# Neighbour sums with features on partitions, scores from one product, R in two rows

## The chip, the cores and the metric

The kernel runs on one core of a Trainium2 chip. The metric is the device time of one execution in microseconds (us), as the median of several runs; profiles come from one further execution that is recorded by the hardware profiler.

## The reference, cut to what matters

A node table `x` (3327 rows of 512 features) goes through four graph layers, each of the form `x = x + layer(relu(layernorm(x)))`. Layers 0, 2 and 3 are graph attention with 8 heads of 64 features. Layer 1 is a GraphSAGE layer.

```python
# attention (layers 0, 2 and 3; layer 0 ends in a batch norm, the others in an ELU)
Wh = h @ W                                  # per head: n x 64
e = leaky_relu(s_i[:, None] + s_j[None, :], 0.2)   # per head, scores of Wh
e = where(adj > 0, e, -9e15)
out = softmax(e, axis=j) @ Wh
# SAGE (layer 1)
mask = adj > 0
agg = mask @ h / maximum(deg, 1)
out = relu(concat([h @ W_self + b_self, agg @ W_nb + b_nb]) @ W_comb + b_comb)
```

The adjacency is sparse and skewed: a few nodes have many neighbours, most have few.

## The kernel before, in words

Nodes are padded to 3328, in 26 blocks of 128 (P) and 52 groups of 64 (GB). The kernel first reads the adjacency and makes, for each group of 64 output nodes, a list of the nodes that are a neighbour of any of them. The lists are cut into chunks of 128 indices: 22 chunks for the first group, then 15, 13, 12, 11, 10 and so on down to 5 and once 4, 359 in all (`CAPS`). Each chunk has a 128 x 64 mask. All sums over neighbours are then products over gathered rows: GpSimd gathers the 128 rows of a chunk from a table in DRAM (`gather`, L1019), and TensorE adds them up in PSUM.

**Attention** (`attend`, three times). exp(leaky_relu(a + b)) is written as a product of a per-node factor and a maximum, so that a weight is max(R_i, r_j), masked. R belongs to the output node and r to the gathered node. For each group, SP fetches one row of R, 8 heads x 64 nodes, into one partition (`fetch`, L1043 and L1044), and `spread` (L1052) copies it to all 128 partitions as a product with a row of ones: 1 x 128 stationary, 1 x 512 moving, f32. A unit is up to three chunks of one group. For each unit VectorE takes the maximum (L1120, into PSUM) and multiplies by the mask (L1127), and TensorE makes 8 products per chunk (L1141), one per head: the weights, 128 x 64, are stationary, the gathered values, 128 x 65 (64 features and a one that sums the weights), are moving. Two heads go to the two halves of the output partitions. In `attend` the orders of TensorE, VectorE and ScalarE are those of the code (`manual_schedule`); GpSimd and SP are ordered by the framework, and outside `attend` all engines are. After each unit `later()` moves older groups on and calls `tick` once.

**The projection of the next layer** makes the table: per block of 128 nodes, the normed block is transposed (p_ps, L710, with four relu activations into hT, L713), two score products follow (p_sd: L717 has hT stationary and 8 columns of WA moving and puts nodes on partitions, L719 has WA stationary and hT moving and puts the 8 heads on partitions, as R needs them), then h @ W (p_wh, L731). The row of a node is 8 x 65 values and 8 factors r. R is clamped, passed through exp, and written to `r_dram`, heads x nodes. `Projection` does this at the start, beside the reading of the adjacency (L593, L595, L597, with the scores in one PSUM bank, `sd`). `Following` does it beside SAGE (for layer 2) and beside attention 2 (for layer 3): `norm` in three steps and `rest` in four, and each `tick` makes one step of the oldest block that is ready. Its PSUM tiles rotate through two banks beside SAGE and through one beside attention 2.

**SAGE**: for each chunk, one product (L1376) has the mask, 128 x 64, stationary and the gathered row, 128 x 512, moving; the two groups of a block fill the two halves of the output partitions, nodes x features. ScalarE casts the masks (L1357). `ending` then works in steps, one per tick: ScalarE scales by one over the degree (s_ag, L1315), TensorE transposes the block with four products (a_ps, L1319) and ScalarE copies it (aT, L1321); TensorE multiplies by the folded weights (n_ps, L1325); VectorE adds the node's own part (L1330), applies relu and adds x (L1331), SP writes the result, and the projection's `begin` takes the block.

The lines that a sentence can't say:

```python
        if self.ready and next(self.ready[0], None) is None:
            self.ready.pop(0)
...
                nc.tensor.matmul(acc[u * GB : (u + 1) * GB, :], m, z, start=f, stop=l)
...
                    nc.tensor.matmul(rb, ones[0:1, :], rrs.pop(g), start=True, stop=True)
```

Of the kernel before, what the change touches and what calls it, by code (L numbers as in the profile page):

```python
# [23 lines left out]
F32 = mybir.dt.float32  # L24
BF16 = mybir.dt.bfloat16
I32 = mybir.dt.int32
I8 = mybir.dt.int8
U8 = mybir.dt.uint8
U16 = mybir.dt.uint16
AF = mybir.ActivationFunctionType  # L30
ALU = mybir.AluOpType
# [5 lines left out]
P = 128  # L37
H = 8
F = 64
D = H * F  # L40
KC = D // P
# [7 lines left out]
GB = 64  # L49
# [10 lines left out]
SMALL = 53.0  # L60
# [510 lines left out]
class Projection:  # L571
# [15 lines left out]
    def block(self, c):  # L587
# [4 lines left out]
        for kc in range(KC):  # L592
            nc.tensor.matmul(sd[:, :H], hT[:, kc, :], WA[wl][:, kc, H:], start=(kc == 0), stop=(kc == KC - 1))  # L593
        for kc in range(KC):
            nc.tensor.matmul(sd[:H, P : 2 * P], WA[wl][:, kc, :H], hT[:, kc, :], start=(kc == 0), stop=(kc == KC - 1))  # L595
        for kc in range(KC):
            nc.tensor.matmul(wh, hT[:, kc, :], self.Wt[:, kc, :], start=(kc == 0), stop=(kc == KC - 1))  # L597
        row = pp.tile([P, ROW], F32, name="v_row", tag="v_row", bufs=3)
        V = row[:, : H * (F + 1)].rearrange("p (h f) -> p h f", f=F + 1)
        nc.scalar.activation(V[:, :, F : F + 1], sd[:, :H].rearrange("p (h o) -> p h o", o=1), AF.Exp)  # L600
        nc.scalar.activation(row[:, H * (F + 1) :], sd[:, :H], AF.Exp, scale=-0.8, bias=self.cs["down"])

        rr = pp.tile([H, P], F32, name="r_row", tag="r_row", bufs=2)
        nc.vector.tensor_scalar(rr, sd[:H, P : 2 * P], -SMALL, SMALL, ALU.max, ALU.min)
        nc.scalar.activation(rr, rr, AF.Exp, scale=0.8, bias=self.cs["down"][:H])
        n = P // GB
        nc.sync.dma_start(
            self.r_dram[c * n : (c + 1) * n, :, :].rearrange("g h i -> h g i"), rr.rearrange("h (g i) -> h g i", i=GB)
        )
# [42 lines left out]


class Following:

# [14 lines left out]
    def tick(self):  # L670
        if self.ready and next(self.ready[0], None) is None:
            self.ready.pop(0)
        for g in list(self.early):
            hx = next(g)
            if hx is not None:
                self.early.remove(g)
                self.ready.append(self.rest(*hx))
# [28 lines left out]
    def rest(self, c, hx):  # L706
# [9 lines left out]
        for kc in range(KC):  # L716
            nc.tensor.matmul(sd[:, :H], hT[:, kc, :], WA[wl][:, kc, H:], start=(kc == 0), stop=(kc == KC - 1))  # L717
        for kc in range(KC):
            nc.tensor.matmul(sd[:H, P : 2 * P], WA[wl][:, kc, :H], hT[:, kc, :], start=(kc == 0), stop=(kc == KC - 1))  # L719
        row = pp.tile([P, ROW], F32, name="v_row", tag="v_row", bufs=2)  # L720
        V = row[:, : H * (F + 1)].rearrange("p (h f) -> p h f", f=F + 1)
        nc.scalar.activation(V[:, :, F : F + 1], sd[:, :H].rearrange("p (h o) -> p h o", o=1), AF.Exp)
        nc.scalar.activation(row[:, H * (F + 1) :], sd[:, :H], AF.Exp, scale=-0.8, bias=self.cs["down"])
        rr = pp.tile([H, P], F32, name="r_row", tag="r_row", bufs=2)
        nc.scalar.copy(rr, sd[:H, P : 2 * P])  # L725
        yield True

        nc.vector.tensor_scalar(rr, rr, -SMALL, SMALL, ALU.max, ALU.min)  # L728
        wh = self.psum.tile([P, D], F32, name="p_wh", tag="p_ps", bufs=self.pb)
        for kc in range(KC):  # L730
            nc.tensor.matmul(wh, hT[:, kc, :], self.Wt[:, kc, :], start=(kc == 0), stop=(kc == KC - 1))  # L731
        yield True
        nc.scalar.activation(rr, rr, AF.Exp, scale=0.8, bias=self.cs["down"][:H])
        n = P // GB
        nc.sync.dma_start(
            self.r_dram[c * n : (c + 1) * n, :, :].rearrange("g h i -> h g i"), rr.rearrange("h (g i) -> h g i", i=GB)
        )
        for h in range(H):
            nc.scalar.mul(V[:, h, 0:F], wh[:, h * F : (h + 1) * F], V[:, h, F : F + 1])  # L739
        nc.sync.dma_start(self.table[c * P : (c + 1) * P, :ROW], row.bitcast(I32))  # L740
        yield None

# [248 lines left out]
def sparse(ctx: ExitStack, tc: tile.TileContext, t: dict, out: bass.AP, WA, ls, cs, idx, rdeg, first):  # L991
# [32 lines left out]
    def attend(layer, table, r_dram, finish, tick=lambda: None, home=None):  # L1024
# [11 lines left out]
        with tc.tile_pool(name=f"fatt{layer}", bufs=2) as ap, tc.tile_pool(  # L1036
# [4 lines left out]
            def fetch(g):  # L1041
                if g < ls.G:
                    rr = ap.tile([1, H * GB], F32, name="r_one", tag="r_one", bufs=3)  # L1043
                    nc.sync.dma_start(rr, r_dram[g : g + 1, :, :].rearrange("g h i -> g (h i)"))  # L1044
                    rrs[g] = rr

            def spread(g):


                if g < ls.G:  # L1050
                    rb = aps.tile([P, H * GB], F32, name="r_bc", tag="r_bc", bufs=2)
                    nc.tensor.matmul(rb, ones[0:1, :], rrs.pop(g), start=True, stop=True)  # L1052
                    rbs[g] = rb.rearrange("p (h i) -> p h i", i=GB)
# [99 lines left out]
    def following(lx, layer, wl, W, pb=1):  # L1153

        table = dram.tile([NP, ROW], I32, name=f"table{layer}")
        r_dram = dram.tile([ls.G, H, GB], F32, name=f"r_dram{layer}")
        pp = lx.enter_context(tc.tile_pool(name=f"fproj{layer}", bufs=1))
        pps = lx.enter_context(tc.tile_pool(name=f"fproj_ps{layer}", bufs=1, space=PSUM))
        return Following(tc, cs, N, wl, W, WA, table, r_dram, pp, pps, pb)
# [24 lines left out]
    with ExitStack() as mx:  # L1184
# [128 lines left out]
        def ending(b, acc):  # L1313
            ag = gp.tile([P, D], F32, name="s_ag", tag="s_ag")
            nc.scalar.mul(ag, acc, rdeg[:, b : b + 1])  # L1315
            yield
            tp = gps.tile([P, KC, P], F32, name="a_ps", tag="a_ps")
            for kc in range(KC):
                nc.tensor.transpose(tp[:, kc, :], ag[:, kc * P : (kc + 1) * P], cs["ident"])  # L1319
            aT = gp.tile([P, KC, P], F32, name="aT", tag="aT")  # L1320
            nc.scalar.copy(aT, tp)  # L1321
            yield
# [6 lines left out]
            o = gp.tile([P, D], F32, name="s_o", tag="s_o", bufs=3)  # L1329
            nc.vector.tensor_tensor(o, ps, y[:, b, :], ALU.add)  # L1330
            nc.vector.scalar_tensor_tensor(o, o, 0.0, xr, ALU.max, ALU.add)  # L1331
# [16 lines left out]
        def load(i):  # L1348
# [3 lines left out]
            for u, kn in enumerate(parts[i][1]):  # L1352
                if kn is not None:
# [4 lines left out]
                    for k in range(n):  # L1358
                        gather(zt[:, k, :], h_dram, k0 + k)
                        zs.append((k, u, k0 + k, mf[:, k, :], zt[:, k, :]))  # L1360
            zs.sort(key=lambda x: x[:2])
# [3 lines left out]
        for i, (b, _, begins, stops) in enumerate(parts):  # L1365
            load(i + SAHEAD)
            if begins:
                acc = gps.tile([P, D], F32, name="sage_acc", tag="sage_acc")
            at = -1
            for r, u, k, m, z in loaded.pop(i):  # L1370
                if r != at:
                    at = r
                    tick()
                g = b * PG + u
                f, l = k == ls.first[g], k == ls.first[g] + CAPS[g] - 1
                nc.tensor.matmul(acc[u * GB : (u + 1) * GB, :], m, z, start=f, stop=l)  # L1376
            if stops:
# [14 lines left out]
def gnn_stack(tc: tile.TileContext, t: dict, out: bass.AP):  # L1392
    with ExitStack() as ctx:
# [8 lines left out]
        table = ldram.tile([NP, ROW + NP // WB // 2], I32, name="table0")  # L1402
        r_dram = ldram.tile([ls.G, H, GB], F32, name="r_dram0")
        idx = kp.tile([P, ls.n], I32, name="idx")
# [73 lines left out]
```

## Time and profile before

| what | value |
|---|---|
| median of 3 runs | 2994.06 us (2988.13 to 3010.09) |
| the profiled execution | 3035.44 us, its span 3033.2 us |
| busy over the span: PE, VectorE, ScalarE, GpSimd | 77%, 59%, 35%, 45% |
| mean granted clock of TensorE | 0.788 of full |
| gathers for attention, L1019 | 1077, 952 ns each, 1025.4 us |
| gathers for SAGE, L1019 | 359, 950 ns each, 341.2 us |
| maximum and mask, L1120 and L1127 | 405 each, 639.5 and 638.3 us |
| h @ W beside other work, p_wh L731 | 416 records, 215.3 us |
| n_ps L1325 | 208 records, 106.7 us |
| scores, p_sd L717 and L719 | 416 records each, 72.5 and 75.9 us |
| transposes p_ps L710 and a_ps L1319 | 208 and 104 records, 326 and 337 ns each |

In the profile's rows an engine is PE (TensorE's products), PEld (its weight loads), DVE (VectorE), ACT (ScalarE), POOL (GpSimd) or SP (which only issues transfers). A row of a group says: line, engine, operation, output <- inputs, for a product the shapes "stationary rows * stationary columns, moving rows x moving columns", the count, then busy time, mean ns of one, and the idle time of the engine just before, with what ended it. Ends of products are modelled by the profiler, and products overlap, so the busy time of a group is shorter than count x mean. A row of the waits says: engine, line, what it waited for, us in total, times, longest. A row of the timeline begins with start and length in us and ends with the idle time before, where there was one.

### The profile page before, as it was taken

Reading aid. Unit: us, or ns where it says so; the run is one execution under the profiler, and the core shown is the slowest. Engines: PE = TensorE matmul, PEld = TensorE weight load, DVE = VectorE, ACT = ScalarE, POOL = GpSimd, SP = SyncE. Lnnn points to the kernel's source line nnn. Section 1 sums busy time; section 2 is a strip of 40 time slices with the busy share of each in tenths; the row PEclk is TensorE's granted clock in tenths of the full one; section 3 lists DMA queues with packets and bytes.
Section 4 is the critical chain, followed back from the end, with each engine's and each line's share of the span. In section 5 each row is a group of like instructions: output and inputs, shape, how many; then the busy total and the mean of one; then the engine's idle time right before and its main releaser. Section 6 shows DMA issues by size and latency. Waiting matters only on the chain.

```text
span 3033.2 us, 55483 instructions
## 1 busy us (share of the span) xinstructions
PE 2335.1 (77%) x22046; PEld 1441.9 (48%) x22046; DVE 1797.3 (59%) x2124; ACT 1051.0 (35%) x3857; POOL 1376.2 (45%) x1464
## 2 busy tenths in 40 slices
PE   4767577878787786888988677888889757777775
PEld 2434244555554332333333355555665445656554
DVE  7657577778876910011111277777766367887886
ACT  1223112233334322344444313445666601223333
POOL 1000255556551046666554255555544056565553
PEclk9778788877778898799999767777777766676766
DMA  7563377776662746666655366666655166666664
GB/s 279 186 258 125 133 217 226 235 222 207 201 191 78 248 140 198 195 202 221 202 182 180 114 169 183 186 181 188 185 173 171 56 184 186 188 195 194 200 197 130
DMA packets 186637, 561.52 MB, mean 185 GB/s; under 512 B 35385, under 2 KB 40321, under 8 KB 183044
## 3 DMA queue, kind: packets, MB, share of 16 engines
q0 software_dynamic: 114880, 404.47, 45.4%
q1 hardware_dynamic: 68470, 148.32, 13.8%
q10 hardware_dynamic: 3022, 5.11, 0.5%
q8 instruction: 177, 2.90, 0.4%
q14 instruction: 88, 0.72, 0.1%
HBM read 498.42 MB, written 59.36 MB: 184 GB/s over the span
## 4 chain that ended last, share of the span: by engine, by line
PE 63%; issue 14%; ACT 5%; DVE 2%; another core or an unknown queue 2%; DMA 1%; POOL 1%; SPq 0%; DVEq 0%; ACTq 0%; POOLq 0%
PE facc L1141 29%; PE p_wh L731 7%; PE r_bc L1052 6%; PE sage_acc L1376 5%; PE n_ps L1325 3%; PE p_sd L719 2%; PE p_sd L717 2%; PE s_ps L1300 2%; PE fwx_ps L1218 1%; PE bmean_ps L1228 1%; PE p_ps L710 1%; ACT v_row L739 1%; POOL rows L1019 1%; PE a_ps L1319 1%
## 5 line engine op out<-in xcount | busy, mean ns | idle before, releaser
L1019 POOL DMA_INDIRECT rows<-table,idx x1077 | 1025.4, 952 | 1231.6 <-PE facc L1141 362.4
L1141 PE MATMUL facc<-rows,wgt 128*64 128x65 f32 x17232 | 953.3, 270 | 380.9 <-issue 342.1
L1141 PEld LDWEIGHTS facc<-rows,wgt 128*64 128x64 f32 x17232 | 826.1, 178 | 669.3 <-issue 556.4
L1127 DVE TENSOR_TENSOR wgt<-mx,mask 128x1536 f32<-128x1536 f32 (+1 forms) x405 | 638.3, 1576 | 174.4 <-PE facc L1141 82.4
L1120 DVE TENSOR_TENSOR mx<-r_bc,rows 128x1536 f32<-128x1536 f32 (+1 forms) x405 | 639.5, 1579 | 163.9 <-PE facc L1141 75.9
L1019 POOL DMA_INDIRECT z_rows<-h_dram,idx x359 | 341.2, 950 | 392.0 <-ACT hT L1297 139.2
L1079 ACT ACTIVATE fhp<-sums,rd 64x64 f32<-64x64 f32 x832 | 219.7, 334 | 146.9 <-DVE rd L1073 85.2
L1052 PE MATMUL r_bc<-r_one,fones 1*128 1x512 f32 x312 | 220.9, 793 | 15.8 <-DMA r_one<-r_dram 9.3
L731 PE MATMUL p_wh<-fWt,hT 128*128 128x512 f32 x416 | 215.3, 664 | 1.8 <-ACT r_row L725 1.8
L1376 PE MATMUL sage_acc<-z_rows,z_mask 128*64 128x512 f32 x718 | 208.4, 635 | 10.6 <-issue 6.2
L1069 ACT COPY sums<-facc 128x260 f32<-128x260 f32 x156 | 57.5, 368 | 405.8 <-PE facc L1141 344.9
L728 DVE TENSOR_SCALAR r_row<-r_row 8x128 f32<-8x128 f32 x52 | 11.8, 228 | 301.7 <-ACT r_row L725 183.7
L1112 ACT ACTIVATE mask<-on 128x192 uint8<-128x192 uint16 (+1 forms) x135 | 46.5, 344 | 394.9 <-DVE on L1106 202.6
L1330 DVE TENSOR_TENSOR s_o<-n_ps,bn_y 128x512 f32<-128x512 f32 x26 | 17.9, 687 | 209.9 <-PE n_ps L1325 185.4
L731 PEld LDWEIGHTS p_wh<-fWt,hT 128*128 128x128 f32 x416 | 85.3, 216 | 107.4 <-issue 101.6
L597 PE MATMUL wh_ps<-fWt,hT 128*128 128x512 f32 x208 | 124.7, 731 | 2.5 <-DVE v_row L610 2.5
L739 ACT ACTIVATE v_row<-p_wh,v_row 128x64 f32<-128x64 f32 x416 | 89.8, 322 | 80.4 <-PE p_wh L731 70.3
L1325 PE MATMUL n_ps<-fWx,aT 128*128 128x512 f32 x208 | 106.7, 651 | 5.1 <-ACT aT L1321 3.4
L1079 ACT ACTIVATE bn_y<-sums,rd 64x64 f32<-64x64 f32 x416 | 109.5, 333 | 2.4 <-DVE rd L1073 0.5
L1376 PEld LDWEIGHTS sage_acc<-z_rows,z_mask 128*64 128x64 f32 x718 | 51.0, 140 | 116.6 <-issue 103.0
L1300 PE MATMUL s_ps<-fWx,hT 128*128 128x512 f32 x208 | 95.8, 615 | 9.2 <-ACT hT L1297 9.2
L713 ACT ACTIVATE hT<-p_ps 128x128 f32<-128x128 f32 x208 | 54.6, 277 | 123.2 <-PE facc L1141 82.8
(191 smaller groups left out, 2153.8 us busy)
## 6 DMA issues: line engine op xcount, KB each, us to landing
adj_i<-in_adj SPq DMA_DIRECT2D x26, 1664.0 KB
table<-v_row SPq DMA_DIRECT2D x78, 264.0 KB
rows<-table,idx POOLq DMA_INDIRECT x1077
fin_x<-fx SPq DMA_DIRECT2D x52, 256.0 KB
ln_x<-in_x SPq DMA_DIRECT2D x26, 256.0 KB
bn_x<-in_x SPq DMA_DIRECT2D x13, 512.0 KB
fx<-bn_x SPq DMA_DIRECT2D x13, 512.0 KB
fsage_x<-fx SPq DMA_DIRECT2D x26, 256.0 KB
```

Of the source, the lines that this page charges most:

```text
L597: nc.tensor.matmul(wh, hT[:, kc, :], self.Wt[:, kc, :], start=(kc == 0), stop=(kc == KC - 1))
L731: nc.tensor.matmul(wh, hT[:, kc, :], self.Wt[:, kc, :], start=(kc == 0), stop=(kc == KC - 1))
L739: nc.scalar.mul(V[:, h, 0:F], wh[:, h * F : (h + 1) * F], V[:, h, F : F + 1])
L1019: nc.gpsimd.indirect_dma_start(out=dst, out_offset=None, in_=src[:, :], in_offset=bass.IndirectOffsetOnAxis(ap=idx[:, k : k + 1], axis=0))
L1052: nc.tensor.matmul(rb, ones[0:1, :], rrs.pop(g), start=True, stop=True)
L1079: nc.scalar.mul(hp[o0 : o0 + GB, h * F : (h + 1) * F], sm[mine, q, 0:F], rd[mine, q, :])
L1120: nc.vector.tensor_tensor(mx[:, :n], rbs[g].unsqueeze(1).to_broadcast(full), gt[:, :n, H * (F + 1) : ROW].unsqueeze(3).to_broadcast(full), ...
L1127: nc.vector.tensor_tensor(wt[:, :n], mx[:, :n], mk.unsqueeze(2).to_broadcast(full), ALU.mult)
L1141: nc.tensor.matmul(accs[g][v * GB : (v + 1) * GB, q * (F + 1) : (q + 1) * (F + 1)], wt[:, k, h, :], gt[:, k, h * (F + 1) : (h + 1) * (F + 1)],
L1300: nc.tensor.matmul(ps, hT[:, kc, :], Wx[:, 0, kc, :], start=(kc == 0), stop=(kc == KC - 1))
L1325: nc.tensor.matmul(ps, aT[:, kc, :], Wx[:, 1, kc, :], start=(kc == 0), stop=(kc == KC - 1))
L1376: nc.tensor.matmul(acc[u * GB : (u + 1) * GB, :], m, z, start=f, stop=l)
```

## The change

1. **SAGE's sums.** The gathered row is now stationary, four times 128 x 128, and the mask moving, 128 x 64; the sum comes out with features on partitions and nodes along the free dimension. The transposes of `ending` and the scaling in ScalarE are gone; the sum is copied from PSUM and used as it is. One over the degree is applied behind the product with the weights, where nodes are on partitions again, in the VectorE step that adds the node's own part.
2. **Scores.** One product with all 16 columns of WA gives both scores with nodes on partitions. R is clamped and passed through exp there, and split into two parts (`halves`): the value in TensorE's reduced f32 form, and what remains of it. A product with the identity transposes both, 128 x 16 to 16 x 128, and they are written to `r_dram`, which has two rows for each group now.
3. **R's spread.** `fetch` brings two rows to two partitions, and `spread` adds them up as it copies them, 2 x 128 ones by 2 x 512, both read as the reduced f32 form (`float32r`).
4. **Steps.** `rest` has six steps in place of four. A tick makes up to two steps when two blocks are ready, and begins the next block when one ends.

```diff
@@ Projection.block
-            nc.tensor.matmul(sd[:, :H], hT[:, kc, :], WA[wl][:, kc, H:], start=(kc == 0), stop=(kc == KC - 1))
-        for kc in range(KC):
-            nc.tensor.matmul(sd[:H, P : 2 * P], WA[wl][:, kc, :H], hT[:, kc, :], start=(kc == 0), stop=(kc == KC - 1))
+            nc.tensor.matmul(sd[:, : 2 * H], hT[:, kc, :], WA[wl][:, kc, :], start=(kc == 0), stop=(kc == KC - 1))
...
+        sf = pp.tile([P, H], F32, name="s_col", tag="s_col", bufs=2)
+        nc.vector.tensor_scalar(sf, sd[:, :H], -SMALL, SMALL, ALU.max, ALU.min)
+        rs = halves(nc, pp, self.cs, sf)
+        nc.tensor.transpose(sd[: 2 * H, P : 2 * P], rs(), self.cs["ident"])
+        rr = pp.tile([2 * H, P], F32, name="r_row", tag="r_row", bufs=2)
+        nc.scalar.copy(rr, sd[: 2 * H, P : 2 * P])
...
+def halves(nc, pool, cs, sf):
+    rf = pool.tile([P, H], F32, name="r_full", tag="r_full", bufs=2)
+    rs = pool.tile([P, 2, H], F32, name="r_half", tag="r_half", bufs=2)
+    nc.scalar.activation(rf, sf, AF.Exp, scale=0.8, bias=cs["down"])
+    nc.scalar.copy(rs.bitcast(F32R)[:, 0, :], rf)
+
+    def other():
+        nc.vector.tensor_tensor(rs.bitcast(F32R)[:, 1, :], rf, rs[:, 0, :], ALU.subtract)
+        return rs.rearrange("p t h -> p (t h)")
+
+    return other
...
@@ Following.tick
-        if self.ready and next(self.ready[0], None) is None:
-            self.ready.pop(0)
+        for _ in range(min(2, len(self.ready))):
+            while self.ready and next(self.ready[0]) is None:
+                self.ready.pop(0)
@@ Following.rest
...
+        rs = halves(nc, pp, self.cs, sf)
         for h in range(H):
             nc.scalar.mul(V[:, h, 0:F], wh[:, h * F : (h + 1) * F], V[:, h, F : F + 1])
         nc.sync.dma_start(self.table[c * P : (c + 1) * P, :ROW], row.bitcast(I32))
+        yield True
+        tr = self.psum.tile([2 * H, P], F32, name="p_tr", tag="p_ps", bufs=self.pb)
+        nc.tensor.transpose(tr, rs(), self.cs["ident"])
+        yield True
+        rr = pp.tile([2 * H, P], F32, name="r_row", tag="r_row", bufs=2)
+        nc.scalar.copy(rr, tr)
...
@@ attend
-                    rr = ap.tile([1, H * GB], F32, name="r_one", tag="r_one", bufs=3)
-                    nc.sync.dma_start(rr, r_dram[g : g + 1, :, :].rearrange("g h i -> g (h i)"))
+                    rr = ap.tile([2, H * GB], F32, name="r_two", tag="r_two", bufs=3)
+                    nc.sync.dma_start(rr, r_dram[g, :, :, :].rearrange("t h i -> t (h i)"))
...
-                    nc.tensor.matmul(rb, ones[0:1, :], rrs.pop(g), start=True, stop=True)
+                    nc.tensor.matmul(rb, ones[0:2, :].bitcast(F32R), rrs.pop(g).bitcast(F32R), start=True, stop=True)
@@ SAGE, ending
-            ag = gp.tile([P, D], F32, name="s_ag", tag="s_ag")
-            nc.scalar.mul(ag, acc, rdeg[:, b : b + 1])
-            yield
-            tp = gps.tile([P, KC, P], F32, name="a_ps", tag="a_ps")
-            for kc in range(KC):
-                nc.tensor.transpose(tp[:, kc, :], ag[:, kc * P : (kc + 1) * P], cs["ident"])
             aT = gp.tile([P, KC, P], F32, name="aT", tag="aT")
-            nc.scalar.copy(aT, tp)
+            nc.scalar.copy(aT, acc)
...
-            nc.vector.tensor_tensor(o, ps, y[:, b, :], ALU.add)
+            nc.vector.scalar_tensor_tensor(o, ps, rdeg[:, b : b + 1], y[:, b, :], ALU.mult, ALU.add)
@@ SAGE, sums
-                nc.tensor.matmul(acc[u * GB : (u + 1) * GB, :], m, z, start=f, stop=l)
+                for kc in range(KC):
+                    nc.tensor.matmul(
+                        acc[:, kc, u * GB : (u + 1) * GB],
+                        z[:, kc * P : (kc + 1) * P],
+                        m,
+                        start=begins,
+                        stop=(stops and kc == KC - 1 and (r, u) == last),
+                    )
+                    begins = False
```

## The prediction

> **What bounds the kernel now.** I read the page first: how full each engine is, then the chain of work that ended last, then the groups the change touches.
>
> ```profile
> span 3033.2 us, 55483 instructions
> ...
> PE facc L1141 29%; PE p_wh L731 7%; PE r_bc L1052 6%; PE sage_acc L1376 5%; PE n_ps L1325 3%; PE p_sd L719 2%; PE p_sd L717 2%; PE s_ps L1300 2%; PE fwx_ps L1218 1%; PE bmean_ps L1228 1%; PE p_ps L710 1%; ACT v_row L739 1%; POOL rows L1019 1%; PE a_ps L1319 1%
> ...
> L1141 PE MATMUL facc<-rows,wgt 128*64 128x65 f32 x17232 | 953.3, 270 | 380.9 <-issue 342.1
> ...
> L1052 PE MATMUL r_bc<-r_one,fones 1*128 1x512 f32 x312 | 220.9, 793 | 15.8 <-DMA r_one<-r_dram 9.3
> ...
> L1376 PE MATMUL sage_acc<-z_rows,z_mask 128*64 128x512 f32 x718 | 208.4, 635 | 10.6 <-issue 6.2
> ```
>
> TensorE (PE) rows head the chain, among them every product the change rewrites. An f32 product shows as two records: 156 R rows give x312. Then busy time by stage (first projection; attention 0; norm and own product; SAGE; attention 2; attention 3):
>
> ```profile
> 0.00:354.00 354.00, 236.08 (x1504) 140.89 (x1504) 235.99 (x448) 79.84 (x352) 9.57 (x28) 0.84 0.51 188
> 354.00:951.00 597.00, 456.61 (x5980) 305.86 (x5980) 457.12 (x463) 178.34 (x621) 340.01 (x359) 0.77 0.69 212
> 951.00:1123.00 172.00, 139.23 (x378) 63.05 (x378) 103.55 (x202) 55.43 (x97) 20.80 (x22) 0.91 0.48 162
> 1123.00:1713.00 590.00, 495.24 (x1749) 207.32 (x1749) 57.78 (x159) 239.77 (x991) 320.36 (x337) 0.90 0.60 186
> 1713.00:2426.00 713.00, 574.78 (x6589) 393.88 (x6587) 480.79 (x480) 336.39 (x1278) 343.08 (x359) 0.76 0.57 167
> 2426.00:3033.00 607.00, 433.18 (x5848) 330.86 (x5848) 462.13 (x374) 161.27 (x520) 342.32 (x359) 0.67 0.64 184
> ```
>
> After the two times come PE, weight load, VectorE, ScalarE and GpSimd busy, PE's clock, DMA share, GB/s. SAGE is PE's stage (495 of 590). Attention has no full engine, so I read PE's own waits there, in attention 3 (the line's gaps end by "issue", nothing visible):
>
> ```profile
> PE facc L1141 <- issue: 135.4, 267, 2.6
> PE facc L1141 <- DVE wgt L1127: 7.6, 2, 6.6
> ```
>
> PE hardly waits for VectorE; its 433 busy and 135 of gaps make up the stage. Last, PE's order in one late SAGE block:
>
> ```profile
> 1577.60 0.60 PE L710 MATMUL p_ps<-fident,ln_h 128*128 128x128 f32 x4
> 1578.13 1.08 PE L1376 MATMUL sage_acc<-z_rows,z_mask 128*64 128x512 f32 x4
> 1579.14 3.70 PE L1325 MATMUL n_ps<-fWx,aT 128*128 128x512 f32 x8
> 1582.67 0.95 PE L717 MATMUL p_sd<-WA,hT 128*128 128x8 f32 x8
> 1583.56 1.04 PE L719 MATMUL p_sd<-hT,WA 128*8 128x128 f32 x8
> 1584.53 1.08 PE L1376 MATMUL sage_acc<-z_rows,z_mask 128*64 128x512 f32 x4
> 1585.54 3.70 PE L731 MATMUL p_wh<-fWt,hT 128*128 128x512 f32 x8
> 1589.17 2.79 PE L1376 MATMUL sage_acc<-z_rows,z_mask 128*64 128x512 f32 x12
> 1597.09 1.11 PE L1319 MATMUL a_ps<-fident,s_ag 128*128 128x128 f32 x4 [5.12 <-ACT s_ag L1315]
> ```
>
> Rates follow: sage_acc (2.79 - 1.08) / 8 = 0.214 us a record; n_ps starts 3.53 before the next product, 0.44 a record. The same 512 columns cost sage_acc half, because two groups of 64 columns run side by side. p_sd L717 takes 0.89 / 8 = 0.11.
>
> **What the Trainium skill says.** "TensorE: Matmul & The Clock Gate", section "LDWEIGHTS (loading the stationary operand)": the load costs about columns / 1.2 ns, so 107 ns for 128; L717, with only 8 columns moving, shows 0.11. The same page, "Step-by-step: what each phase is for": weight loads are pulled ahead of running matmuls; the trace agrees for 512 moving columns (0.44 is all moving time), none shows it for a 128-column load under 64. "FP8 and Floating Point Precision", "TensorE Precision Notes": true FP32 takes four passes, a reduced form reads FP32 as FP22. No row here shows that form.
>
> **The change, part by part.** All sums are against the profiled 3035.44 us (span 3033.2); the median of the runs is 41 lower, and I carry the difference over.
>
> 1. R spread (L1052), 52 per attention. Now 220.9 / 156 = 1.42 us each. One pass of four is an estimate of 0.36, with 0.1 for a fixed part, assumed, 0.45: saved 0.97 x 156 = 151 us of PE. Ends: 0 (it runs as now) and 1.15 each, 180. How much reaches the stage? Attention 2 does 115 + 86 + 19 = 220 us of projection products more than attention 3 and is 106 longer: 0.48. Attention 0 has 96 us of L1209, L1218 and L1228 more and is 10 shorter: 0. PE's waits say nearly 1. I take 0.65, -98; ends 0 and -180. VectorE's idle 140, 232 and 145 us leave room.
>
> 2. Scores in one product. L719 goes: 416 records, 75.9 us, split like the p_sd busy of the stages (59 and 86): 30 in SAGE, 45 in attention 2. L717 keeps its price, since loading sets it. One transpose a block comes back, at L710's 0.33 about 9 us a stage. Attention 2: (45 - 9) x 0.65 = -23.
>
> 3. The longer projection, six steps for four, two a tick when two blocks stand ready. In attention 2 PE's order is fixed by hand; in the changed order 17 blocks have the transposes directly before the scores, which then wait for four hT activations, 1.15 us in the trace, some 1.5 with latency (3.5 if ScalarE is inside the 2.14 us of L1079). Behind stand an R row and 24 facc products, which VectorE waits for. 17 x 1.5 x 0.65 = +17; ends 0 and +60. One block more is left for the tail, with one PSUM bank: 0.66 + 1.15 + 0.95 + 0.7 + 3.7 + 1.75 + 0.6, about +10. ScalarE, VectorE and SP gain small steps per block (0.2 to 0.3 each); ScalarE is at 240 of 590 and 336 of 713, so nothing; uncovered they are 1 us x 52.
>
> 4. SAGE's sums. Now 718 records side by side; then 359 x 4 x 2 = 2872 with 128-column loads: at 0.11 each 316 against 208, +108. Gone: 104 transposes, 22, and L719's 30; back: 9. Net +65. Two covers: the first two blocks hold 62 gathers, 62 x (0.95 + 0.30) = 78 us of GpSimd, more than their new PE work (62 x 8 x 0.11, and 8.4 of n_ps, p_wh, p_sd and p_ps a block, 71), so what they add (55, less 35 side-by-side pairs of 0.86) vanishes there, 24; and the transposes' waits for s_ag (41.7 us over 11, one shown above) go, since in the new order two chunks stand between the copy and n_ps. I count half, 21. Net +20; ends -30 and, if loads don't hide, +155. The fused VectorE step keeps 0.69.
>
> 5. First projection. PE loses 36 us (L595), but the stage waits on adjacency loads and VectorE's 3.6 us masks; the new chain clamp, exp, copy, subtract, transpose holds the sd bank longer. +5; ends -15 and +30. R's DMAs grow to 8 KB a block and 4 KB a fetch, under transfers of 264 KB: nothing; uncovered, a fetch a group late by some 0.1, 16 us.
>
> Sum: -98 - 23 + 17 + 10 + 20 + 5 = -69.
>
> **The rivals.** (A) Slower: weight loads don't hide under 64 columns, so a record costs 0.107 + 0.053 = 0.16: 2872 x 0.053 = 152, of which some 135 shows; 3060. For: no such pair in the trace. Against: facc, with 64-column loads, at times runs 96 records in 2.95 us, 0.031 each, which leaves no room for load and pass in turn. It decides from 0.135 a record on. (B) The gaps swallow it: facc's "issue" gaps come back as the R row shrinks, or the reduced product isn't shorter (the change then doesn't do what it says). The 187 us of parts 1 and 2 count 0.15 instead of 0.65, +93: 3018. For: attention 0 against 3. Against: the chain. (C) PE's saving counts in full and SAGE loses its waits: -187 + 26 + 10 - 15 = -166, 2828.
>
> **How the numbers follow.** Forecast 0.46, A 0.15, B 0.19, C 0.20. The likeliest is 2994 - 69 = 2925, its own range 2885 to 2970. The 8-in-10 range, 2838 to 3035, leaves out most of A and half of C. About 1% (30 us) is what a measurement of this kernel can tell from no change: faster 0.38 of the forecast and all of C, 0.58; same 0.08 and half of B, 0.17; slower A and half of B, 0.25.
>
> **What would show it.** R rows at x156 near 0.45 us, with the attention stages 20 to 45 shorter each; sage_acc at x2872 with busy near 316 and SAGE near 610; no wait for s_ag; in attention 2 some 1.5 us of PE idle before p_sd. A sage_acc pitch above 0.135, or facc gaps well over 342, would make the forecast wrong.

## The result, and the profile after

The changed kernel takes 3083.62 us, the kernel before 3000.98 beside it: ratio 1.028, 95% interval 1.023 to 1.033. It is 83 us slower where 69 us faster was forecast. First the page of the changed kernel: the span, TensorE's rows at the head of the chain of waits, and two groups.

```profile
span 3080.5 us, 58331 instructions
...
PE facc L1168 28%; PE sage_acc L1398 12%; PE p_wh L751 8%; PE n_ps L1346 4%; PE r_bc L1079 3%; PE p_sd L738 2%; PE s_ps L1327 2%; PE bmean_ps L1255 1%; PE fwx_ps L1245 1%; ACT fhp L1106 1%; ACT v_row L755 1%; PE p_ps L731 1%; ACT hT L734 1%; DMA fWc<-in_L_gnn_W_comb 1%
...
L1168 PE MATMUL facc<-rows,wgt 128*64 128x65 f32 x17232 | 982.3, 269 | 405.7 <-issue 378.8
...
L1398 PE MATMUL sage_acc<-z_mask,z_rows 128*128 128x64 f32 x2872 | 386.7, 296 | 12.2 <-issue 11.3
```

On the chain sage_acc went from 5% to 12% and R's spread from 6% to 3%. The 2872 records of sage_acc take 386.7 us, 71 more than forecast, and the gaps of facc grew from 342.1 to 378.8. The stages of the same execution follow (columns as in the prediction: length; busy PE, weight load, VectorE, ScalarE, GpSimd; clock, DMA share, GB/s), and then SAGE's row of the kernel before, cut at the same events:

```profile
0.00:302.80 302.80, 187.51 (x1298) 114.11 (x1298) 225.16 (x458) 87.92 (x403) 9.58 (x28) 0.84 0.58 216
302.80:912.50 609.70, 432.09 (x5953) 299.20 (x5953) 469.59 (x480) 180.10 (x623) 340.41 (x359) 0.79 0.69 211
912.50:1074.40 161.90, 130.86 (x365) 61.60 (x365) 100.62 (x199) 53.19 (x93) 15.14 (x16) 0.90 0.47 158
1074.40:1780.10 705.70, 651.86 (x3627) 513.82 (x3626) 63.55 (x186) 239.02 (x1021) 326.51 (x343) 0.84 0.53 158
1780.10:2477.30 697.20, 511.39 (x6351) 369.31 (x6352) 483.14 (x506) 340.71 (x1328) 342.36 (x359) 0.77 0.60 171
2477.30:3080.50 603.20, 415.48 (x5804) 337.35 (x5804) 462.03 (x374) 161.94 (x521) 343.97 (x359) 0.64 0.66 186
```

```profile
1116.20:1711.40 595.20, 500.44 (x1762) 209.93 (x1760) 58.47 (x160) 238.64 (x984) 322.26 (x339) 0.91 0.60 185
```

Cut at these events (first mean_ps of each layer, first var_ps, start of the last stretch of s_ps), the profile of before has 334.0, 619.2, 163.0, 595.2, 710.4 and 611.4 us. So SAGE lost 110, the first projection won 31, and the three attentions 31 together. The execution profiled before is 41 us slower than its median, and the fourth set of runs below gives the attentions only 13. SAGE's row holds the surprise: PE 151 us busier, and its clock 0.84 where it was 0.91.

The runs below were made in five sets, in which the kernel before took 2998, 2998, 2577, 3033 and 2577 us, and these levels do not follow the chip, since the chip of the first set and that of the fifth have the same number on record. Every ratio is to the kernel before in the same set. Stages are compared within a set, or between the two sets of 2998 where the text says so. The changed kernel itself was run with the result (3001 for the kernel before) and in the fourth set.

### The profile page after: what moved, and what is told of

Read it like the earlier page. It is cut to its first block, busy times and chain, and to the rows that moved or that the text cites. A ratio compares the mean times of both kernels' runs of the same rounds, so it can differ in the third digit from the quotient of the medians.

```text
span 3080.5 us, 58331 instructions
## 1 busy us (share of the span) xinstructions
PE 2329.2 (76%) x23394; PEld 1695.4 (55%) x23394; DVE 1804.1 (59%) x2202; ACT 1062.9 (35%) x3987; POOL 1378.0 (45%) x1464
## 4 chain that ended last, share of the span: by engine, by line
PE 64%; issue 14%; ACT 6%; DVE 2%; another core or an unknown queue 1%; DMA 1%; POOL 0%; SPq 0%; DVEq 0%; ACTq 0%
PE facc L1168 28%; PE sage_acc L1398 12%; PE p_wh L751 8%; PE n_ps L1346 4%; PE r_bc L1079 3%; PE p_sd L738 2%; PE s_ps L1327 2%; PE bmean_ps L1255 1%; PE fwx_ps L1245 1%; ACT fhp L1106 1%; ACT v_row L755 1%; PE p_ps L731 1%; ACT hT L734 1%; DMA fWc<-in_L_gnn_W_comb 1%
## 5 line engine op out<-in xcount | busy, mean ns | idle before, releaser
L1168 PE MATMUL facc<-rows,wgt 128*64 128x65 f32 x17232 | 982.3, 269 | 405.7 <-issue 378.8
L1398 PEld LDWEIGHTS sage_acc<-z_mask,z_rows 128*128 128x128 f32 x2872 | 380.8, 213 | 28.7 <-issue 28.2
L1398 PE MATMUL sage_acc<-z_mask,z_rows 128*128 128x64 f32 x2872 | 386.7, 296 | 12.2 <-issue 11.3
L751 PE MATMUL p_wh<-fWt,hT 128*128 128x512 f32 x416 | 241.1, 732 | 3.1 <-ACT s_col L745 1.4
L1351 DVE SCALAR_TENSOR_TENSOR s_o<-n_ps,rdeg,bn_y 128x512 f32<-128x512 f32 x26 | 19.5, 750 | 242.3 <-PE n_ps L1346 190.7
L751 PEld LDWEIGHTS p_wh<-fWt,hT 128*128 128x128 f32 x416 | 96.5, 243 | 115.9 <-issue 110.8
L738 PE MATMUL p_sd<-WA,hT 128*128 128x16 f32 x416 | 85.4, 322 | 58.5 <-ACT hT L734 45.7
L1378 ACT CAST z_mask<-mask 128x128 f32<-128x128 uint8 (+1 forms) x196 | 53.8, 295 | 206.8 <-PE sage_acc L1398 180.9
L738 PEld LDWEIGHTS p_sd<-WA,hT 128*128 128x128 f32 x416 | 82.0, 271 | 78.1 <-ACT hT L734 53.8
L1346 PE MATMUL n_ps<-fWx,aT 128*128 128x512 f32 x208 | 118.1, 710 | 6.4 <-issue 6.1
```

The costliest lines, as they stand in the source:

```text
L738: nc.tensor.matmul(sd[:, : 2 * H], hT[:, kc, :], WA[wl][:, kc, :], start=(kc == 0), stop=(kc == KC - 1))
L1168: nc.tensor.matmul(accs[g][v * GB : (v + 1) * GB, q * (F + 1) : (q + 1) * (F + 1)], wt[:, k, h, :], gt[:, k, h * (F + 1) : (h + 1) * (F + 1)],
L1346: nc.tensor.matmul(ps, aT[:, kc, :], Wx[:, 1, kc, :], start=(kc == 0), stop=(kc == KC - 1))
L1398: nc.tensor.matmul(acc[:, kc, u * GB : (u + 1) * GB], z[:, kc * P : (kc + 1) * P], m, start=begins, stop=(stops and kc == KC - 1 and (r, u ...
```

## The experiments

**First set: the parts by themselves** (kernel before: 2998 us). Theory S: the rewritten sums are the whole loss. Theory G: what attention's products save comes back as gaps.

SAGE's new sums alone:

```diff
 # the kernel before, with this and the new ending, nothing else
-acc[u * GB : (u + 1) * GB, :], m, z
+acc[:, kc, u * GB : (u + 1) * GB], z[:, kc * P : (kc + 1) * P], m
```

> The kernel before with SAGE's new sums and ending alone; scores, R and ticks as before. Theory S (the rewritten sums are the loss: twice the TensorE records per pair of groups, at a lower granted clock): SAGE's stage grows from about 589 to about 700 us, nothing else moves, ratio to before 1.03 to 1.04. Rival T (the two steps per tick and the longer projection crowd SAGE): SAGE under 620 us, ratio under 1.012.

Measured: 1.038 (1.034 to 1.041), 113 us by the ratio; SAGE 715.5 us. The sums alone bring the whole loss; T falls.

Everything but them:

```diff
 # the changed kernel, with
-acc[:, kc, u * GB : (u + 1) * GB], z[:, kc * P : (kc + 1) * P], m
+acc[u * GB : (u + 1) * GB, :], m, z      # and the ending of before
```

> The changed kernel with SAGE's sums and ending as before; all other parts of the change kept. Theory S: SAGE back at 580 to 590 us, the gains of the other stages kept (some 31 in the first projection, 31 in the three attentions), so 55 to 70 us faster than before, ratio 0.977 to 0.982. Rival T: SAGE stays near 680 or more, ratio over 1.01. The forecast's own sum without its SAGE term: 89 us faster, 0.970.

Measured: 0.990 (0.987 to 0.993); SAGE back at 589.7. That is 1% faster than the kernel before, half of what S wanted: against the first run, in the same set, attention 0, 2 and 3 stand at 609.9, 692.3 and 602.7 where that has 609.3, 696.7 and 602.6, so only the first projection kept its gain.

R's reduced spread alone:

```diff
 # the kernel before, with
-nc.tensor.matmul(rb, ones[0:1, :], rr, ...)
+nc.tensor.matmul(rb, ones[0:1, :].bitcast(F32R), rr.bitcast(F32R), ...)
```

> The kernel before with only the product that spreads R read in the reduced f32 form, one row as before; the part of R that the reduced form drops is left out of the sums. The forecast: TensorE's saving counts at 0.65, some 30 us in each attention, ratio 0.967. Theory G (the attention stages are paced by something that is not TensorE's work, so its savings come back as gaps): about 10 us in each attention, 20 to 40 in all, ratio 0.987 to 0.993. The bare saving does nothing: ratio 0.998 or more.

Measured: 0.993 (0.990 to 0.997), G's size, but in another place: attention 2 is 677.5, 19 less than in the first run, attention 0 and 3 are 605.8 and 602.0, within 4.

Scores and steps alone:

```diff
 # all but SAGE's sums, with
-nc.tensor.matmul(rb, ones[0:2, :].bitcast(F32R), rr.bitcast(F32R), ...)
+nc.tensor.matmul(rb, ones[0:2, :], rr, ...)
```

> The kernel before with only the scores from one product, the longer projection and the new ticks; R stands in two rows, but is spread by an f32 product as before, and SAGE's sums are as before. If the 31 us that the first projection lost came from its shorter TensorE work: that stage near 303 us, ratio 0.985 to 0.990, attention as before within 10 us. If it was a matter of that execution alone (adjacency loads), the stage stays near 334 and the ratio is 0.995 to 1.005.

Measured: 0.997 (0.996 to 0.999). The first projection is 302.3 against 328.4, as expected of its shorter TensorE work, but the ratio is not: attention 2 takes 712.5, 16 more than in the first run and outside the 10 us expected.

**Second set: the clock, and what paces attention** (2998 us). A mask of 128 columns:

```diff
 # the changed kernel; z_mask is [P, SUNIT, PG, GB]
+nc.vector.memset(mf[:, :n, 1 - u, :], 0.0)
-acc[:, kc, u * GB : (u + 1) * GB],
+acc[:, kc, :],
```

> The changed kernel, but the mask of each group is 128 columns wide, the other group's half zero (VectorE writes the zeros), so each of SAGE's products moves 128 columns and adds to both halves. Records and weight loads as in the changed kernel, the sums too. Theory C (part of SAGE's loss is the clock, which is granted lower when little moves through the array): SAGE's clock rises from 0.84 towards 0.90 and its stage falls from 700 by 30 to 60 us, ratio to before 1.008 to 1.018. Theory N (only the number of records and their loads counts): stage and ratio as in the changed kernel, 1.025 to 1.032. If moving 128 columns doesn't fit under a load: stage over 730, ratio over 1.038.

Measured: 1.013 (1.009 to 1.017), SAGE 656.1, clock 0.94. Twice the columns, the same sums, records and weight loads, and 50 us less than the changed kernel had with the result (46 by the ratios): theory C. TensorE's busy time in SAGE fell by 61 us, only 20 of them in sage_acc; the rest is in the other products of the stage. Its first three eighths, in the changed kernel and then here (after the length comes TensorE's busy time with its records):

```profile
1080.00:1168.00 88.00, 82.12 (x437) 73.91 (x435) 3.06 (x8) 13.06 (x52) 45.73 (x49) 0.67 0.52 150
1168.00:1255.00 87.00, 79.76 (x459) 67.83 (x458) 4.96 (x14) 22.78 (x98) 48.92 (x52) 0.76 0.60 173
1255.00:1342.00 87.00, 79.06 (x462) 65.66 (x461) 6.90 (x19) 25.99 (x108) 45.00 (x48) 0.82 0.56 168
```

```profile
1080.00:1161.00 81.00, 66.57 (x455) 59.30 (x454) 7.38 (x35) 14.45 (x58) 46.65 (x50) 0.89 0.55 163
1161.00:1242.00 81.00, 72.49 (x487) 60.10 (x485) 8.96 (x40) 22.18 (x92) 49.24 (x52) 0.96 0.65 193
1242.00:1324.00 82.00, 71.76 (x444) 58.74 (x444) 10.99 (x46) 27.98 (x120) 43.57 (x46) 0.92 0.59 180
```

TensorE is busier in the changed kernel (93% against 82% in the first eighth), yet has the lower clock and does fewer records per us. In one stretch it is busy without a break for 44 us, at half clock:

```profile
1094.80:1139.00 44.20, 44.20 (x198) 42.13 (x197) 0.00 (x0) 4.20 (x14) 26.94 (x29) 0.50 0.61 173
```

TensorE's timeline shows what that means for the other products of the stage, in the changed kernel and then with the wide mask:

```profile
1342.53 6.09 PE L751 MATMUL p_wh<-fWt,hT 128*128 128x512 f32 x8
1348.45 0.78 PE L1398 MATMUL sage_acc<-z_mask,z_rows 128*128 128x64 f32 x6
1349.07 3.65 PE L1346 MATMUL n_ps<-fWx,aT 128*128 128x512 f32 x8
1352.56 0.27 PE L759 MATMUL p_tr<-fident,r_half 128*16 128x128 f32 x1
1352.66 10.34 PE L1398 MATMUL sage_acc<-z_mask,z_rows 128*128 128x64 f32 x89
```

```profile
1342.31 4.01 PE L751 MATMUL p_wh<-fWt,hT 128*128 128x512 f32 x8
1346.16 1.95 PE L1399 MATMUL sage_acc<-z_mask,z_rows 128*128 128x128 f32 x16
...
1353.17 0.27 PE L759 MATMUL p_tr<-fident,r_half 128*16 128x128 f32 x1
1353.28 5.52 PE L1399 MATMUL sage_acc<-z_mask,z_rows 128*128 128x128 f32 x48
1358.64 0.60 PE L731 MATMUL p_ps<-fident,ln_h 128*128 128x128 f32 x4
```

After the short products h @ W (p_wh) runs at a granted clock of 0.50 until 1347.3, and takes 5.92 us to the next start instead of 3.85. In the last rows of both the clock is 1.00: there a record of 64 columns takes 10.34 / 89 = 0.116 us, one of 128 columns (1358.64 - 1353.28) / 48 = 0.112. So 64 more moving columns cost no time under a 128-column load.

R's spread in eight pieces:

```diff
 # all but SAGE's sums, with
-nc.tensor.matmul(rb, ones..., rr, start=True, stop=True)
+for h in range(H):
+    s = slice(h * GB, (h + 1) * GB)
+    nc.tensor.matmul(rb[:, s], ones..., rr[:, s], start=True, stop=True)
```

> All of the change but SAGE's sums (ratio 0.990), and R's reduced spread cut into eight products of 64 columns for each group: 7 products and 7 weight loads more, 728 instructions of TensorE in each attention, at nearly the same work. Theory F (the attention stages are paced by the supply of TensorE's instructions, about 51 ns for each product or load: 602 us for 11,608 of them in attention 3, 610 for 11,906 in attention 0): some 37 us in each attention, 80 to 110 in all, ratio 1.017 to 1.028. Theory G (paced by gathers and buffers): attention 0 and 3 within 8 us of 610 and 603, ratio 0.990 to 0.998. Theory P (TensorE's work): 8 loads of 0.11 for 0.63, 13 us in each at most, ratio up to 1.003.

Measured: 1.004 (1.002 to 1.005), some 41 us over all but SAGE's sums. Against the last run of this set, attention 0 and 3 are 12 and 9 us longer, not 37; attention 2 is 30 longer than in all but SAGE's sums (first set). Theory F falls as it stood (51 ns for every instruction). But the work did not stay nearly the same: a piece took 0.17 us (216.3 / 1248), and R's row in attention 3 grew from 33.5 to 75.2 us. The run added work and instructions together and doesn't tell one from the other.

Pairs of heads:

```diff
 # all but SAGE's sums; 4 products a chunk
-accs[g][v * GB : (v + 1) * GB, 65 columns of h], wt[:, k, h, :], gt[:, k, 65 of h]
+accs[g][:, q * P : (q + 1) * P], wt[:, k, 2 * q : 2 * q + 2, :], gt[:, k, 128 from 130 * q]
```

> All of the change but SAGE's sums, and in attention two heads share a product: both heads' weights stationary, 128 columns, and 128 moving columns, so 4 products (8 records, 8 loads) a chunk in place of 8 (16 and 16). It leaves out two of the 130 columns of each pair, the second head's last feature and its sum of weights (the first head's sum, held between bounds, divides both); both heads' cross terms are computed and not used. Work per record grows from 0.03 to 0.06 to about 0.11 us, so TensorE's busy time stays near that of the kernel without it or grows. Theory F: instructions halve, the stages fall until VectorE or GpSimd bounds them, 500 to 550 us for attention 0 and 3, ratio under 0.95. Theory G: no change of these stages beyond 10 us, ratio 0.985 to 1.0. Theory P: no gain or a loss.

Measured: 0.955 (0.952 to 0.959). Attention 0 and 3 fell to 578.8 and 571.9, not to 550. TensorE's busy time didn't shrink (430 in attention 3, against 405 in the last run of this set), but its clock went from 0.68 to 0.88 and facc's gaps there from 169 to 116. Two causes are mixed here, fewer instructions and more columns.

The first projection and the spread:

```diff
 # the kernel before, with Projection.block and spread of the changed one; in Following.rest, steps and ticks of before,
+nc.scalar.copy(r2.bitcast(F32R)[:, 0, :], rr)
+nc.vector.tensor_tensor(r2.bitcast(F32R)[:, 1, :], rr, r2[:, 0, :], ALU.subtract)
```

> The kernel before with two parts of the change alone: the first projection's scores from one product, and R's reduced spread. Beside SAGE and attention 2 the projection keeps its two score products, four steps and old ticks; R is split into its two rows where it lies, by a copy and a subtraction on 8 partitions. If the longer projection and its ticks cost attention 2 some 15 us (692 with them, 677 without, both with the reduced spread): 40 to 55 us faster than before, ratio 0.982 to 0.987, attention 2 at 675 to 683. If they cost nothing: like all of the change but SAGE's sums, ratio 0.990.

Measured: 0.986 (0.979 to 0.992), attention 2 at 686.9, between the two expectations. It has the lowest ratio of the complete versions, but its interval overlaps that of all but SAGE's sums: the longer projection would cost attention 2 some 5 us by this run (692.3 - 686.9, across two sets), 15 to 16 by pairs of the first set.

**Third set.** The kernel before took 2577 us here. Half the gathers' bytes:

```diff
 # all but SAGE's sums
-table = dram.tile([NP, ROW], I32, ...)
+table = dram.tile([NP, H // 2 * (F + 1) + H], I32, ...)
```

> All of the change but SAGE's sums, and in attention 2 and 3 (not 0) the table's rows and each gather are 268 values wide in place of 528. It leaves out the values of heads 4 to 7 (those of heads 0 to 3 are used twice) and takes eight values of head 4 in place of r; every instruction stays. Theory D (TensorE's gaps in attention come from transfers that the gathers' bytes hold up, its own instructions among them): gaps of facc in attention 3 fall from 159 us to under 110, the stage from 603 to under 575, attention 2 likewise, ratio under 0.972. Otherwise: attention 3 at 595 to 605, ratio 0.983 to 0.992. Attention 0 is the control, 610 in both.

Measured: 1.004, attention 3 at 514.3 with VectorE 461 busy: here VectorE sets the pace, and the run tells nothing of D. Three pairs:

```diff
 # the first projection and the spread, with
+accs[g][:, 130 columns], wt[:, k, h : h + 2, :], gt[:, k, 130 of h]   # h = 0, 2, 4; heads 6, 7 as before
```

> The first projection's scores from one product and R's reduced spread (ratio 0.986), and in attention the first six heads as three products with two heads' weights stationary (128 columns) and 130 columns moving, the last two heads as before: 10 records a chunk in place of 16, nothing left out (the sums of three pairs and of the last one fill 455 columns of the bank; three small reciprocals in place of one). The run with four pairs gained 31 us in each attention at half the records; three pairs should give two thirds to three quarters of it: 60 to 75 us in all, ratio 0.960 to 0.967. If VectorE's two small steps more and the 455 columns to copy instead of 260 take it back: ratio over 0.975.

Measured: 1.040 (1.037 to 1.042), slower where 3 to 4% faster was expected: facc is 439.6 us busy in attention 3, where the kernel of half gathers has 263.7. Its 3590 records take 0.122 us each, the 5744 of the other 0.046: fewer records, but dearer by more. Narrow pairs:

```diff
 # pairs of heads, with
-accs[g][:, q * P : (q + 1) * P], ..., gt[:, k, 128 from 130 * q]
+accs[g][:, q * P : q * P + 65], ..., gt[:, k, 65 of 2 * q]
```

> The kernel with pairs of heads (four products of 128 stationary columns a chunk), but only the first head's 65 columns move in each: same records, loads and instructions, half of what moves. It leaves out the second head's values (the first head's are used for both). Theory C (the clock is granted by how much moves through the array): attention's clock falls from 0.88 to 0.89 back to 0.80 or less and the stages lengthen, attention 3 from 572 to 580 to 600. Theory I (the pairs gained by having fewer instructions): the stages at 572 or less, ratio at or under 0.955.

Measured: 1.176 (1.171 to 1.180), attention 3 at 696.8 with a clock of 0.51: theory C, and fewer instructions alone win nothing. Reduced SAGE:

```diff
 # the changed kernel
-z[:, kc * P : (kc + 1) * P], m
+z[:, kc * P : (kc + 1) * P].bitcast(F32R), m.bitcast(F32R)
```

> The changed kernel, but SAGE's products read gathered rows and mask in the reduced f32 form: it leaves out what that form drops of h. One record in place of two, 1436 in place of 2872. Theory N (the rest of SAGE's loss is the records of the new form, 0.11 to 0.135 us each): some 150 to 190 us less work for TensorE, SAGE falls from 700 to between 560 and 600, where gathers and the other products bound it, ratio to before 0.98 to 0.99. If a reduced record costs as much as two (the 128-column load counts twice): SAGE stays at 680 or more, ratio over 1.02.

Measured: 1.016 (1.014 to 1.018). SAGE takes 515.6, where half gathers, with the old sums, has 495.8: at half the records the new form is still 20 us longer. Its sage_acc is 231.0 busy in 1436 records, 0.161 each, the clock 0.78 where the old sums have 0.98. The number of records is not the whole price. The changed kernel was not run at this level, so what the reduced form saved isn't known.

**Fourth set: everything side by side** (3033 us).

> The kernel before, for its stages on the chip of the other runs of this call. Ratio 1.000 within 0.3%.

Measured: 1.000.

> The changed kernel on the same chip. If the kernel before takes near 3000 us: ratio 1.025 to 1.032, SAGE 100 to 115 us longer. If it takes near 2580: SAGE's loss should be there too, since it is TensorE's own work and clock: SAGE 80 to 130 us longer; R's saving counts for nothing where VectorE bounds attention (467 us busy of some 515), so ratio 1.025 to 1.045.

Measured: 1.023 (1.021 to 1.024).

> All of the change but SAGE's sums, on the same chip. Near 3000 us for the kernel before: ratio 0.987 to 0.993. Near 2580: the first projection 28 us shorter, attention 0 and 3 as before, attention 2 up to 30 us longer from the longer projection's waits: ratio 0.988 to 1.004.

Measured: 0.991 (0.989 to 0.992). The stages of these three runs, in us:

| stage | before | changed | all but SAGE's sums |
|---|---|---|---|
| first projection | 332.5 | 305.5 | 308.6 |
| attention 0 | 619.9 | 618.9 | 617.4 |
| norm and own product | 162.8 | 160.7 | 162.9 |
| SAGE | 594.9 | 705.9 | 609.2 |
| attention 2 | 713.7 | 702.5 | 703.0 |
| attention 3 | 612.0 | 611.4 | 612.1 |

TensorE's groups in attention 3, the kernel before and then all but SAGE's sums:

```profile
L1141 PE MATMUL facc<-rows,wgt 128*64 128x65 f32 x5744 | 364.5, 292 | 138.0 <-issue 129.3 <-DVE wgt L1127 7.2 <-DMA rows<-table,idx 0.5
L1052 PE MATMUL r_bc<-r_one,fones 1*128 1x512 f32 x104 | 86.1, 919 | 6.0 <-DMA r_one<-r_dram 4.7 <-issue 1.1 <-PE facc L1141 0.2
```

```profile
L1168 PE MATMUL facc<-rows,wgt 128*64 128x65 f32 x5744 | 371.6, 284 | 179.4 <-issue 164.9 <-DVE wgt L1154 12.0 <-DVE mx L1147 0.4
L1079 PE MATMUL r_bc<-r_two,fones 2*128 2x512 f32 x52 | 34.1, 658 | 6.9 <-DMA r_two<-r_dram 4.5 <-PE facc L1168 2.4
```

R's row lost 52 us, facc's busy time took 7 and its idle time 41 of them, and the stage stayed at 612.

> As above with half the gathers' width in attention 2 and 3, on the same chip. It leaves out the values of heads 4 to 7 there. Near 3000 us for the kernel before: theory D (TensorE's supply is held up by the gathers' bytes) has attention 3 under 575 us against 603, otherwise 595 to 605. Near 2580: both theories have attention 3 within 5 us of the kernel without it.

Measured: 0.990 (0.988 to 0.993), attention 3 at 612.8 (DMA share 0.39, against 0.64), gaps that end by issue 169.0, against 164.9. Theory D falls.

**Fifth set** (2577 us again). Two kernels of the third set.

> Three pairs of heads, nothing left out, with the first projection's and R's parts of the change. Near 3000 us for the kernel before: 60 to 75 us faster than the 0.986 of those two parts alone would give with attention as it was, ratio 0.955 to 0.970, gaps of facc well under 340 us. Near 2580: slower again, ratio 1.035 to 1.045.

> Pairs of heads with 65 columns moving; the second head's values are left out. Near 3000 us for the kernel before: Theory I (fewer instructions is what the pairs gained): attention 3 at 575 or less, ratio under 0.96. Theory C (the moving columns and the clock they get): attention 3 at 680 to 700 as on the other chip, ratio over 1.03.

Measured: 1.038 (1.036 to 1.040) and 1.176 (1.171 to 1.181), as in the third set. At this level the two runs still show the clock. Attention 3 with 130 columns under a 128-column load (in six records of ten), then with 65 in all:

```profile
2148.20:2676.60 528.40, 462.03 (x3650) 370.30 (x3650) 475.05 (x478) 168.68 (x521) 345.06 (x359) 0.92 0.73 212
```

```profile
2327.90:3026.60 698.70, 664.61 (x2932) 631.67 (x2932) 470.89 (x426) 162.34 (x521) 342.88 (x359) 0.51 0.57 160
```

The second has fewer records and moves half as much in most of them, keeps TensorE 95% busy, and has a mean clock of 0.51 for 700 us.

## Why the prediction was wrong

In the fourth set, where the loss is 70 us, SAGE added 111 where the forecast had 20, the three attentions saved 13 where it had 94, and the first projection saved 27 where it had 5 lost.

**The step that failed most: part 4, SAGE's sums, +20.** They cost +110 to +113. The count (2872) was right, and the price at full clock (0.11, measured 0.116) nearly so. But "at 0.11 each 316" took the full clock for granted: measured were 0.135, and 0.166 in the first eighth. Times the granted clocks of 0.84 and 0.67 that is 0.113 and 0.111, the price at full clock again. So sage_acc took 71 us more than forecast, and the other products of the stage some 16 more by the same sums (an estimate: 151 busier in all, sage_acc 178 of it, so the others fell by 27 and not by 43). The wide mask, which in TensorE's work changes only the columns moved, gave back 50 of the loss. Rival A's 3060 comes nearest to the result, and by luck: its mechanism, loads that don't hide, is refuted by 128 columns taking no longer than 64. The page had the warning: SAGE's clock was 0.90 with 512 columns moving and attention's 0.67 to 0.77 with 65.

The covers: idle time of TensorE did fall, from 595 - 500 = 95 to 54 us, close to the 45 claimed; but busy time grew by 151, not 65, and 151 less 41 is the 110 of this profile. The first cover failed in place: the first two blocks' sums ended 75 us into the stage before and 105 after. Their last gather had ended 8 us earlier before and 24 after, so TensorE, most of that time at half clock, was what the sums waited for.

The Trainium skill, "TensorE: Matmul & The Clock Gate", section "What's actually happening", says that the default is a throttled clock and that activity releases it. The runs show that a busy TensorE, as the profile counts it, is not yet that activity: 44 us without a break at 0.50 in SAGE, and in attention 3 of the fifth set 95% busy at 0.51 with 65 columns under a 128-column load, but 87% busy at 0.92 with 130 in most products. That the columns moved under the same loads raise the clock is shown by the wide mask, and the two attention runs fit; how the chip measures it is not shown.

**Part 1, the spread, -98: size and share both off.** One product takes 0.63 us (97.7 / 156 in the changed kernel's page), 0.44 of the 1.42 and not the quarter assumed, so 123 us were saved, not 151. "I take 0.65" failed: of some 41 us in each, 0 to 4 reach attention 0 and 3 (619.9 to 617.4 and 612.0 to 612.1 in the fourth set) and about half attention 2 (19 and 20 by two pairs of the first set). The forecast had a share of 0 in hand, from attention 0 against 3, and averaged it away. (Cut at the events above, attention 0 is 8 us longer than attention 3 for 96 more of products, not 10 shorter: still a small share.) Rival B's mechanism, gaps that swallow the saving, is what the two rows of facc in the fourth set show.

What paces attention stays open. Shown: not the gathers' bytes. Pairs of heads, fewer instructions with more columns, won 28 to 30 us in attention 0 and 3 at the level of 2998; three pairs lost at 2577, and neither was run at the other level. TensorE's timeline in attention 3, all but SAGE's sums, shows how facc's records come:

```profile
2617.79 1.49 PE L1168 MATMUL facc<-rows,wgt 128*64 128x65 f32 x43 [0.21 <-issue]
2619.62 0.34 PE L1168 MATMUL facc<-rows,wgt 128*64 128x65 f32 x3 [0.34 <-issue]
2620.35 0.37 PE L1168 MATMUL facc<-rows,wgt 128*64 128x65 f32 x5 [0.39 <-issue]
2621.08 0.34 PE L1168 MATMUL facc<-rows,wgt 128*64 128x65 f32 x3 [0.36 <-issue]
```

After a burst of 43 records they come in steps of 0.73 us, a few in each. At the level of 2577 us facc takes 264 us in attention 3 (half gathers), where the same kernel takes 371 in the fourth set, and VectorE, 461 busy of 514, is the bound. A supply of instructions that comes too late or something that holds TensorE back would fit; no run here tells them apart.

**Parts 2 and 3, -23 + 17 + 10: the wait was mis-sized.** Together they cost attention 2 some 15 to 16 us by pairs of the first set. PE's own waits there, in the changed kernel:

```profile
PE p_sd L738 <- ACT hT L734: 40.9, 20, 4.1
PE p_ps L731 <- ACT r_row L762: 19.6, 10, 4.3
...
PE p_tr L759 <- ACT v_row L755: 5.5, 3, 1.8
```

The wait before the scores is 2.0 us, 20 times, for the 1.5 and 17 forecast (6.6 us in all before). The other two were not in the sum: with one bank, the next block's transposes wait for the copy of R's row, 2.0 each. That these waits make up the price is argued; no run changes them alone. Whether the scores' saving reached SAGE is not clear: with the old sums the stage takes 582 to 590 us in the runs of 2998 that have the new scores and 594 in those that don't, but in the fourth set 609 against 595.

**Part 5, the first projection, +5: it won 24 to 31.** The step said that adjacency loads and masks set the stage, and so put TensorE's 36 us at nothing. They count nearly in full: TensorE's busy time fell by 39 and its idle time grew by 8. Scores and steps alone bring the gain; which wait carried it is open. ScalarE's waits, in the profile of before and then in that of the changed kernel:

```profile
ACT v_row L600 <- PE sd_ps L595: 64.3, 24, 5.8
```

```profile
ACT r_row L609 <- PE sd_ps L607: 45.4, 25, 4.0
ACT v_row L601 <- PE sd_ps L595: 38.0, 26, 6.2
```

Before, the exps of V stood behind the second score product (L595), which they don't read. That wait shrank, but the copy of R's row now waits for the new transpose, and ScalarE's waits for this bank grew in sum.

**The range** ended at 3035, below the result. It gave rival A 0.15 and added no case in which SAGE and attention both went wrong, as they did. Of the prediction's own signs of being wrong, facc gaps well over 342 came (379), and the sage_acc pitch stood at its bound (0.135).

## What to carry to other kernels

Price a product by its columns moved as well as by its weight load: here short moving sides under full loads lowered the clock, and with it the speed of the other products of the stage, h @ W included. Where either operand can be the stationary one, try the one with more columns as the moving one. Before counting TensorE's saved time as stage time, ask for a stage in the same profile that already had more work and was no longer; if there is one, expect a share near 0 there.

## What the runs showed of the hardware that was not expected

The same program took 2577 us in two sets of runs and 2998 to 3033 in three, and one number of chip stands for both. SAGE with the old sums took 496 to 498 us at clock 0.98 against 582 to 609 at 0.88 to 0.92, attention 3 (half gathers) 514 against 613; the first projection stayed near 303. What sets the level is not known.

TensorE, busy without a break for 44 us in SAGE, had half its clock throughout. An f32 product of 512 columns that took 1.42 us as two records took 0.63 as one reduced record, with two rows summed in it; cut into eight of 64 columns it took 0.17 each.
